# A decoder on one core: where the pieces of a norm and of an expert choice stand in a written order of matmuls

## The chip, the cores and the metric

The kernel is one launch on one core of a Trainium2 chip. The core has five engines that run side by side: TensorE (PE, matmuls and transposes; its weight loads are shown apart as PEld), VectorE (DVE), ScalarE (ACT), GpSimd (POOL) and SyncE (SP, which issues transfers). Each runs its own instructions in order, and they wait for each other through semaphores. Matmul results land in PSUM[...]; DVE and ACT copy them out[...]. The metric is the device time of the launch in microseconds (us), the median of a few runs.

## What is computed

Eight sequences of 512 tokens of width 256, with a context of 64 tokens each, go through two decoder layers. The change lies in the second one (Layer 1), in its attention over tokens and context, and in the choice of experts that follows:

```python
# Layer 1, second attention: 8 heads of 64, keys and values of the tokens and of the context together
q1, k1, v1 = x1 @ Wq1, x1 @ Wk1, x1 @ Wv1
k2, v2 = x2 @ Wk2, x2 @ Wv2
k, v = concat([k1, k2]), concat([v1, v2])            # 512 + 64 rows
attn = softmax(q1 @ k.T * 64 ** -0.5)
x = layernorm(x + (attn @ v) @ Wo + bo)

# Layer 1, experts: 8 of them, the best two per token
xn = layernorm(x) * gamma + beta
probs = softmax(xn @ router_w.T / 1.5)
w, idx = top_k(probs, 2)
y = silu(xn @ W1[e]) @ W2[e]                          # per expert e
out = sum over the two of w * y, + x                  # then once more: x = layernorm(x + out)
```

All data is float32.

## The kernel before

**Stages.** Layer 0's attentions and its feed-forward come first (0 to about 1500 us), then Layer 1's self-attention (to about 2109 us), the attention with the context (2109 to about 2885 us), the experts (to about 3410 us) and the final norms of the eight sequences (to the end).

**Who sets the order.** A planner orders each engine's instructions: it goes by readiness in its own estimate of the times, and among those that are ready by the order in which the program was written. It also hands out the buffers of a pool when the first writer of a tile is planned, and puts in the waits. Where the program says `tc.manual_schedule(engines={PE})`, PE keeps the written order; in the stage with the context this holds for PE alone. `keep_in_program_order` puts one instruction behind all that is written before it on its engine.

**The stage with the context** (L1531 on) goes over 128 units: sequence b, head pair c (0 to 3), query tile i (0 to 3, 128 rows each). `_pipeline` (L32) walks steps; at step s it calls, in this order, `l1x_scores` for unit s, `l1x_transposes` for unit s - 2, `l1x_values` for unit s - 6 and `l1x_ahead` for unit s. Then it takes one piece of work off the list `put_off`.

- `l1x_scores` (L1124): four products of q and k, one PSUM tile of two banks per head (`s_sc`, two buffers); then for each head DVE's negated row maximum (`nm`, L1138) and ACT's exponential with its row sum (`p`, L1139); then `scaled` (L915): DVE's reciprocal and two multiplications of p by it.
- `l1x_transposes` (L1145): nine transposes of p into three PSUM tiles of one bank (`tP2`, then `tP` twice), and their copies to SBUF with `evac` (L104), which takes DVE and ACT by turns.
- `l1x_values` (L1159): products of values and transposed p into one PSUM tile (`o_pv`), closed at the fourth query tile. After the fourth head pair `out_done` puts two pieces of the output projection (`o_out`) on the list, the second of which ends with `normed` (L206), the layer norm of the sequence. Then it calls `routed` (L1518).
- `l1x_ahead` (L1112): the next head pair's projections: q at i = 0 (`t_qk`, copied by ACT), k at i = 2 (copied by DVE), v at i = 3 (`t_v`, copied by ACT). At i = 1 there is none; there `x_transposed` makes the next sequence's transposed `xT` (c = 2, eight transposes `tT`, two PSUM tiles), or the context's values for two sequences (c = 1).

**PSUM** in this stage: two buffers `s` of two banks, three `t` of one bank, one `o`. All of `tP2`, `tP`, `t_qk`, `t_v`, `tT`, `tZ`, `o_out`, `o_r` and `o_rank` take a `t`.

**The route of a sequence** is what `routed` puts on the list, a piece per step: with the second projection piece `route_norm` (a second layer norm, into `z`, doubling of `xs[b]` and its transfer to `total`), a step with nothing, `route_transposes` (eight transposes `tZ` of z, ACT makes `xnT` of them), `route_odds` (16 small matmuls `o_r`, softmax), `route_picks` (the best two, `greatest` called twice), `route_places` (ranks `o_rank`, and eight indirect transfers of rows to `rows_in` by POOL). `xT` and `xnT` have the same tag, `xT`, in a pool with two buffers. For the last sequence the pieces go on `last_route`, which the pipeline of the experts takes up. After the last but one come `early_blocks` (DVE, tables for the experts) and the first expert's loads.

**A layer norm** (`normed`): per row tile DVE takes statistics (`st`, L213) and aggregates them (`mv`, L214), adds epsilon (`ve`, L215), POOL takes the power (`rs`, L216), and the scaling follows: DVE (L227), or with `on_act` one DVE instruction (L220, into `ve` again) and four of ACT (L224). With `then` given, the scaling is not written at once but put on that list.

Of the kernel before, what the change touches and what calls it, by code (L numbers as in the profile page):

```python
# [11 lines left out]
F32 = mybir.dt.float32  # L12
I32 = mybir.dt.int32
AF = mybir.ActivationFunctionType
ALU = mybir.AluOpType
# [9 lines left out]
NEG = -1.0e30  # L25
LN_EPS = 1e-5
PE = mybir.EngineType.PE
SLOT = 2048
TILES = 2

# [19 lines left out]
def decoder_kernel(ctx: ExitStack, tc: tile.TileContext, a: dict, out: bass.AP):  # L50
# [155 lines left out]
    def normed(dst, r, on_act=False, then=None):  # L206

        st = work.tile([P, NT, 6], F32, tag="st", name="st")
        mv = work.tile([P, NT, 2], F32, tag="mv", name="mv")
        ve = work.tile([P, NT], F32, tag="ve", name="ve")  # L210
        rs = work.tile([P, NT], F32, tag="rs", name="rs")
        for i in range(NT):
            dve.bn_stats(st[:, i, :], r[:, i, :])  # L213
            dve.bn_aggr(mv[:, i, :], st[:, i, :])  # L214
        dve.tensor_scalar(ve, mv[:, :, 1], LN_EPS, None, ALU.add)  # L215
        pool.tensor_tensor(rs, ve, mhalf, ALU.pow)  # L216

        def scaling(held=lambda instruction: instruction):
            if on_act:
                dve.scalar_tensor_tensor(ve, mv[:, :, 0], -1.0, rs, ALU.mult, ALU.mult)  # L220
            for i in range(NT):
                if on_act:
                    held(
                        act.activation(dst[:, i, :], r[:, i, :], AF.Identity, bias=ve[:, i : i + 1], scale=rs[:, i : i + 1])  # L224
                    )
                    continue
                dve.tensor_scalar(  # L227
                    dst[:, i, :], r[:, i, :], mv[:, i, 0:1], rs[:, i : i + 1], ALU.subtract, ALU.mult
                )

        if then is None:
            scaling()
        else:
            then.append(scaling)
# [1 line left out]
    def r_tile():  # L236
        return work.tile([P, NT, D], F32, tag="r", name="r", bufs=1)

    def project_and_norm(b, lhs, w, n, plus, later=None):

        r = r_tile()

        def piece(i2):
            o = u_tile("o_out").rearrange("p (i n) -> p i n", i=2)
            for j in range(2):
                i = 2 * i2 + j
                for c in range(n):
                    pe.matmul(  # L248
                        o[:, j, :],
                        lhsT=lhs[:, c, i * P : (i + 1) * P],  # L250
                        rhs=w[:, c, :],
                        start=(c == 0),
                        stop=(c == n - 1),
                    )
            dve.tensor_tensor(r[:, 2 * i2 : 2 * i2 + 2, :], o, plus[:, 2 * i2 : 2 * i2 + 2, :], ALU.add)
            if i2 == NT // 2 - 1:
                normed(xs[b], r)

        for i2 in range(NT // 2):
            if later is None:  # L260
                piece(i2)
            else:
                later.append(partial(piece, i2))
# [657 lines left out]

    put_off = []

    def l1_scores(b, c, m):
        q, k, _ = live["qkv", b, c]
        s = s_tile("s_sc")
        width = sum(i + 1 for i in GROUPS[m]) * P
        p = ph.tile([P, 2, width], F32, tag=f"p{m}", name="p")
        sums = col("sums", 4)
        at = 0  # L930
        for i in GROUPS[m]:
            n = (i + 1) * P
            for j in range(2):
                h = 64 * j
                pe.matmul(  # L935
                    s[:, j, at : at + n],
                    lhsT=q[h : h + 64, i * P : (i + 1) * P],
                    rhs=k[h : h + 64, 0:n],
                    start=True,
                    stop=True,  # L940
                )
            at += n
        at = 0
        for g, i in enumerate(GROUPS[m]):
            n = (i + 1) * P
            masked_softmax(
                s[:, :, at : at + n], p[:, :, at : at + n], causal[:, S - n : S], n, 1.0 / 8.0, sums, 2 * g
            )
            scaled(p[:, :, at : at + n], sums[:, 2 * g : 2 * g + 2], n)
            at += n  # L950
        live["p", b, c, m] = p
# [19 lines left out]
    def out_done(b, c, o, w, n, plus, then=None):  # L971
        if c == 0:
            live["aT", b] = big_tile("aT")
        aT = live["aT", b]
        evac(aT[:, c, :], o)
        if c == n - 1:
            project_and_norm(b, aT, w, n, plus(), put_off)
            if then:
                then(b)

# [143 lines left out]
    def l1x_scores(b, c, i):  # L1124
        q, k, _ = live["qkv", b, c]
        p = p_tile(S + S2, bufs=4)
        sums = col("sums", 4)
        nm = col("nm", 2)
        ss = [s_tile("s_sc")[:, :, 0:HALF] for _ in range(2)]
        for t in range(2):  # L1130
            for j, s in enumerate(ss):
                h = 64 * j
                at = S2 * (1 - j) + HALF * t
                pe.matmul(  # L1134
                    s[:, t, :], lhsT=q[h : h + 64, i * P : (i + 1) * P], rhs=k[h : h + 64, at : at + HALF], start=True, stop=True
                )
        for j, s in enumerate(ss):
            dve.tensor_reduce(nm[:, j : j + 1], s, AX.XY, ALU.max, negate=True)  # L1138
            act.activation(  # L1139
                p[:, j, :].rearrange("p (t n) -> p t n", t=2), s, AF.Exp, bias=nm[:, j : j + 1], accum_out=sums[:, j : j + 1]  # L1140
            )
        scaled(p, sums, S + S2)
        live["p", b, c, i] = p

    def l1x_transposes(b, c, i):  # L1145
        p = live.pop(("p", b, c, i)).rearrange("p j n -> p (j n)")
        if i == 0:
            live["pt", b, c] = pts[c % 2], ph.tile([P, S], F32, tag="pt2", name="pt2")
        pt, pt2 = live["pt", b, c]
        t = t_tile("tP2")[:, 0, :]  # L1150
        pe.transpose(t, p[:, S : S + P], ident)  # L1151
        evac(pt2[:, i * P : (i + 1) * P], t)
        for j in range(2):
            t = t_tile("tP")
            for k in range(NT):
                pe.transpose(t[:, k, :], p[:, (S + P) * j + k * P : (S + P) * j + (k + 1) * P], ident)  # L1156
            evac(pt[j][:, :, i * P : (i + 1) * P], t)

    def l1x_values(b, c, k):  # L1159

# [56 lines left out]
    def over_i(c):  # L1217
        return c.unsqueeze(1).to_broadcast([P, NT, NE])

    def route_norm(b):  # L1220
        z = keep.tile([P, NT, ROW], F32, tag="zr", name="z")
        normed(z[:, :, 0:D], xs[b])

        dve.tensor_scalar(xs[b], xs[b], 2.0, None, ALU.mult)
        sp.dma_start(out=total[b * S : (b + 1) * S, :].rearrange("(i p) d -> p i d", p=P), in_=xs[b])
        live["z", b] = z

    def route_transposes(b):
        z = live["z", b]
# [35 lines left out]
    def greatest(pick, left):  # L1265
# [6 lines left out]
        dve.tensor_tensor(pick, over_i(rev), over_e(top), ALU.is_equal)  # L1272
        return pick

    def route_picks(b):
        pr = live.pop(("pr", b))
        rest = e_tile("rest")
        picks = [greatest(e_tile("pick0"), pr)]
        dve.scalar_tensor_tensor(rest, picks[0], -2.0, pr, ALU.mult, ALU.add)
        picks.append(greatest(e_tile("pick1"), rest))  # L1280

        picked = work.tile([P, NT + 1, NE], F32, tag="both", name="both", bufs=1)
        pool.memset(picked[:, NT, :], 0.0)
        both, z = picked[:, 0:NT, :], live["z", b]
        dve.tensor_tensor(both, picks[0], picks[1], ALU.add)
        dve.tensor_tensor(z[:, :, D : D + NE], both, pr, ALU.mult)

        tc.keep_in_program_order(dve.tensor_copy(z[:, :, D + NE], tokens_at[:, b * NT : (b + 1) * NT]))
        live["picks", b] = picks, picked
# [226 lines left out]
    AHEAD = 1  # L1516

    def routed(b):  # L1518
        pieces = [partial(f, b) for f in (route_norm, route_transposes, route_odds, route_picks, route_places)]
        if b == NB - 1:  # L1520

            last_route.extend(pieces[:1] + 2 * [nothing] + pieces[1:])
            return

        product = put_off.pop()
        put_off.extend([lambda: (product(), pieces[0]()), nothing] + pieces[1:])
        if b == NB - 2:
            put_off.append(early_blocks)
            put_off.extend(partial(moe_load, n, tables_rows) for n in range(AHEAD))
# [1 line left out]
    with phase("l1_context") as ph, tc.manual_schedule(engines={PE}):  # L1531
        l1x_share(0)
        l1x_context_values(0)
        for what in range(3):
            l1x_project(0, 0, what)
        _pipeline(
            [(b, c, i) for b in range(NB) for c in range(4) for i in range(NT)],
            [(0, l1x_scores), (2, l1x_transposes), (6, l1x_values), (0, l1x_ahead)],
            put_off,
        )  # L1540

# [10 lines left out]
    halves = [h for _ in range(NB // 2) for h in slot("last").rearrange("p (b i d) -> b p i d", b=2, i=NT)]  # L1552
    for b in range(NB):
        sp.dma_start(out=halves[b], in_=total[b * S : (b + 1) * S, :].rearrange("(p i) d -> p i d", p=P))
    for b in range(NB):
        y = ph.tile([P, NT, D], F32, tag="y_out", name="y_out", bufs=4)
        normed(y, halves[b], on_act=True)
        act.dma_start(out=out[b].rearrange("(p i) d -> p i d", p=P), in_=y)


# [89 lines left out]
```

## Time and profile before

| | us |
|---|---|
| median of three runs | 3441.79 (3436.52 to 3451.23) |
| the profiled execution | 3444.91 |
| its span, first to last instruction | 3443.2 |
| busy: PE, DVE, ACT, POOL | 3283.1, 2064.1, 1514.2, 1068.8 |
| stage with the context (2109 to 2885): PE, DVE, ACT busy | 748.2, 536.8, 342.4 |
| of it: maxima (L1138), exponentials (L1139), scaling of p (L920) | 183.3, 189.7, 122.3 |
| of it: copies of 128x512 from `tP`, DVE (L108) and ACT (L110), 128 each | 87.1, 74.2 |
| of it: copies of 128x128 from `tP2`, DVE and ACT, 64 each | 18.0, 17.0 |

A line of the profile's timeline gives start, duration, engine, line, operation, what is written and read, shapes and count; in brackets how long the engine sat idle before it, and who ended that. In the table of windows a line has the stretch and its length, then busy time and count of PE, PEld, DVE, ACT and POOL, then the clock granted to TensorE as a share of full speed, the share of the DMA engines and GB/s.

### The profile page before, as it was taken

How to read it: one execution, taken by the hardware profiler on the slowest of the kernel's cores; microseconds unless marked ns; L12 is line 12 of the kernel's file. 1: busy time of each engine (PE TensorE's matmuls, PEld its weight loads, DVE VectorE, ACT ScalarE, POOL GpSimd, SP SyncE). 2: the span in 40 equal slices, each digit the busy share in tenths (PEclk: the TensorE clock that was granted, in tenths of full speed). 3: DMA queues.
4: the chain of work that ended last, by engine and by line, in shares of the span. 5: the costliest groups of instructions: out<-in, count | busy, mean ns of one | idle time of the engine just before them, and what ended most of it. 6: DMA issues, size and time to landing. Idle time of an engine off the chain costs nothing. (4 is left out here: it accounts for less than half of the span.)

```text
span 3443.2 us, 53163 instructions
## 1 busy us (share of the span) xinstructions
PE 3283.1 (95%) x19574; PEld 2083.5 (61%) x19574; DVE 2064.1 (60%) x6605; ACT 1514.2 (44%) x3140; POOL 1068.8 (31%) x1032
## 2 busy tenths in 40 slices
PE   8999999998999989999999999999999999999995
PEld 3444444446666656666676666555555556888884
DVE  5777777766666467777777775667776764111102
ACT  2444444453343245655556654444444443222222
POOL 3777777762111122222222220011111111222222
PEclk8999999998999999999999999999999999999998
DMA  4011011120000099323233230000000005666674
GB/s 136 27 25 34 24 38 38 41 63 13 2 2 1 1 241 255 57 35 40 38 44 44 38 50 4 4 20 19 23 20 15 15 19 191 188 187 185 187 232 136
DMA packets 166006, 235.00 MB, mean 68 GB/s; under 512 B 26569, under 2 KB 128649, under 8 KB 165746
## 3 DMA queue, kind: packets, MB, share of 16 engines
q1 hardware_dynamic: 139010, 175.83, 16.3%
q0 software_dynamic: 25584, 51.57, 10.5%
q10 hardware_dynamic: 1152, 4.19, 0.3%
q8 instruction: 155, 2.54, 0.3%
q14 instruction: 105, 0.86, 0.1%
HBM read 135.83 MB, written 61.11 MB: 57 GB/s over the span
## 5 line engine op out<-in xcount | busy, mean ns | idle before, releaser
L438 DVE CUSTOM_DVE_ANT_0 scored<-s_sc,decay 128x512 f32<-128x512 f32 x512 | 332.6, 687 | 192.2 <-PE s_sc L433 192.2
L290 ACT ACTIVATE p<-p,nm 128x384 f32<-128x384 f32 (+3 forms) x512 | 282.5, 553 | 259.0 <-DVE nm L279 259.0
L895 POOL DMA_DIRECT2D qk<-turned x256 | 204.1, 1223 | 583.4 <-PE s_sc L935 293.6
L496 ACT ACTIVATE pt<-s_st 128x1024 f32<-128x1024 f32 x256 | 262.0, 1024 | 269.3 <-PE s_st L492 242.8
L920 DVE TENSOR_SCALAR p<-p,rsum 128x576 f32<-128x576 f32 (+4 forms) x768 | 300.4, 434 | 10.2
L1506 DVE TENSOR_SCALAR y<-o_y,share 128x256 f32<-128x256 f32 x71 | 34.2, 484 | 403.1 <-PE o_y L1486 403.1
L1139 ACT ACTIVATE p<-s_sc,nm 128x576 f32<-128x576 f32 x256 | 189.7, 743 | 195.2 <-DVE nm L1138 173.5
L1469 PE MATMUL s_h<-xnT,we 128*128 128x256 f32 (+1 forms) x1248 | 258.8, 361 | 0.0
L279 DVE CUSTOM_DVE_ANT_0 p<-s_sc,tabs 128x384 f32<-128x384 f32 (+3 forms) x512 | 225.1, 484 | 46.4 <-PE s_sc L935 44.3
L1486 PE MATMUL o_y<-we,h 128*128 128x256 f32 x1136 | 251.4, 379 | 0.0
L1486 PEld LDWEIGHTS o_y<-we,h 128*128 128x128 f32 x1136 | 215.3, 190 | 29.0
L1507 POOL DMA_INDIRECT total<-y,to x71 | 110.3, 1553 | 385.7 <-DVE y L1506 172.2
L1469 PEld LDWEIGHTS s_h<-xnT,we 128*128 128x128 f32 x1248 | 215.4, 190 | 23.9 <-ACT xnT L1448 0.2
L1138 DVE TENSOR_REDUCE nm<-s_sc 128x1 f32<-128x576 f32 x256 | 183.3, 749 | 77.7 <-PE s_sc L1134 76.6
L110 ACT COPY pt<-tP 128x512 f32<-128x512 f32 (+1 forms) x224 | 110.0, 491 | 216.7 <-PE tP L1151 119.3
L935 PE MATMUL s_sc<-qk 64*128 64x384 f32 (+3 forms) x1024 | 179.4, 462 | 15.5 <-DMA qk<-turned 10.3
L968 ACT COPY pt<-tP 128x384 f32<-128x384 f32 (+1 forms) x384 | 167.0, 527 | 56.1 <-PE tP L967 55.9
L967 PEld LDWEIGHTS tP<-ident,p 128*128 128x128 f32 x1280 | 141.3, 141 | 52.3 <-issue 30.8
L1134 PE MATMUL s_sc<-k,q 64*128 64x288 f32 x1024 | 166.3, 437 | 3.3 <-ACT p L1139 3.1
L967 PE MATMUL tP<-ident,p 128*128 128x128 f32 x1280 | 163.2, 278 | 3.4 <-ACT pt L968 2.4
L433 PE MATMUL s_sc<-k,q 32*128 32x512 f32 x1024 | 156.7, 654 | 3.0 <-ACT k L418 1.5
L450 DVE TENSOR_SCALAR_CACHE_REDUCE diag<-scored,mx 128x128 f32<-128x128 f32 x512 | 155.8, 342 | 0.0
(281 smaller groups left out, 6444.9 us busy)
## 6 DMA issues: line engine op xcount, KB each, us to landing
we<-in_mo_w SPq DMA_DIRECT2D x78, 1024.0 KB
rows_in<-zero SPq DMA_DIRECT2D x64, 530.0 KB
qk<-turned POOLq DMA_DIRECT2D x256, 128.0 KB, 4.6
coef<-in_ff_upw SPq DMA_DIRECT2D x40, 256.0 KB
coef<-in_ff_dnw SPq DMA_DIRECT2D x40, 256.0 KB
xr<-rows_in SPq DMA_DIRECT2D x32, 265.0 KB
x<-in_x SPq DMA_DIRECT2D x8, 512.0 KB
total<-x SPq DMA_DIRECT2D x8, 512.0 KB
```

What stands on the lines that cost most here:

```text
L279: dve.tensor_tensor_reduce(out=p[:, j, 0:n], in0=s[:, j, 0:n], in1=m, scale=-scale, scalar=3.0e38, op0=ALU.add, op1=ALU.min, accum_out=nm[ ...
L290: act.activation(p[:, j, 0:n], p[:, j, 0:n], AF.Exp, bias=nm[:, j : j + 1], scale=-1.0, accum_out=sums[:, at + j : at + j + 1],)
L438: dve.tensor_tensor_reduce(out=scored[:, h, :], in0=s[:, j, :], in1=decay[:, i, :], scale=1.0, scalar=-3.0e38, op0=ALU.mult, op1=ALU.max, ...
L496: tc.keep_in_program_order(act.activation(pt, s, AF.Exp, scale=1.0 / 16.0))
L895: pool.dma_start(out=qk[h : h + 32], in_=other[g : g + 32], accum_op=ALU.add)
L920: dve.tensor_scalar(p[:, j, 0:n], p[:, j, 0:n], rsum[:, j : j + 1], None, ALU.mult)
L935: pe.matmul(s[:, j, at : at + n], lhsT=q[h : h + 64, i * P : (i + 1) * P], rhs=k[h : h + 64, 0:n], start=True, stop=True,)
L967: pe.transpose(t[:, n, :], p[:, j, at * P : (at + 1) * P], ident)
L1138: dve.tensor_reduce(nm[:, j : j + 1], s, AX.XY, ALU.max, negate=True)
L1139: act.activation(p[:, j, :].rearrange("p (t n) -> p t n", t=2), s, AF.Exp, bias=nm[:, j : j + 1], accum_out=sums[:, j : j + 1])
L1469: pe.matmul(s[:, j, :], lhsT=w1[:, c, f * P : (f + 1) * P], rhs=xnT[:, c, :], start=(c == 0), stop=(c == KC - 1),)
L1486: pe.matmul(o, lhsT=h[:, f, i * P : (i + 1) * P], rhs=w2[:, f, :], start=(f == 0), stop=(f == 7),)
```

## The change

Nothing is computed otherwise, and the number of matmuls, copies and transfers stays. What moves:

- `project_and_norm` and `route_norm` hand `normed` a list, so that the scalings are pieces of their own. `routed` puts more pieces on the list: scaling of `xs[b]`, `route_norm` (statistics of z alone), scaling of z, transposes together with the doubling of `xs[b]` (`route_twice`), odds, the first choice (`route_pick`), the second, places. For the last sequences some are joined again.
- `scaled` is a stage of its own, `l1x_scaled`, for unit s - 1.
- ACT copies `tP2` and the first `tP`, DVE the second, in each step.
- In a step `l1x_ahead` comes before `l1x_values`.
- In the final norms DVE keeps the written order, and the scaling of a sequence is written after the statistics of the next.
- `scaling` passes its DVE multiplications through `held`, as it did ACT's; `route_scale` gives `keep_in_program_order` for it, so these multiplications stand behind all DVE work that is written before them.

```diff
                     continue
-                dve.tensor_scalar(
-                    dst[:, i, :], r[:, i, :], mv[:, i, 0:1], rs[:, i : i + 1], ALU.subtract, ALU.mult
+                held(
+                    dve.tensor_scalar(
+                        dst[:, i, :], r[:, i, :], mv[:, i, 0:1], rs[:, i : i + 1], ALU.subtract, ALU.mult
+                    )
                 )
...
-    def project_and_norm(b, lhs, w, n, plus, later=None):
+    def project_and_norm(b, lhs, w, n, plus, later=None, then=None):
...
-                normed(xs[b], r)
+                normed(xs[b], r, then=then)
...
+    then_scaled = None
...
-            project_and_norm(b, aT, w, n, plus(), put_off)
+            project_and_norm(b, aT, w, n, plus(), put_off, then_scaled)
...
+        live["p", b, c, i] = p, sums
+
+    def l1x_scaled(b, c, i):
+        p, sums = live["p", b, c, i]
         scaled(p, sums, S + S2)
-        live["p", b, c, i] = p
...
-        evac(pt2[:, i * P : (i + 1) * P], t)
+        act.copy(pt2[:, i * P : (i + 1) * P], t)
...
-            evac(pt[j][:, :, i * P : (i + 1) * P], t)
+            (act.copy, dve.tensor_copy)[j](pt[j][:, :, i * P : (i + 1) * P], t)
...
+    then_scaled = []
+
+    def route_scale(b):
+        then_scaled.pop(0)(tc.keep_in_program_order)
+
     def route_norm(b):
         z = keep.tile([P, NT, ROW], F32, tag="zr", name="z")
-        normed(z[:, :, 0:D], xs[b])
+        normed(z[:, :, 0:D], xs[b], then=then_scaled)
+        live["z", b] = z
+
+    def route_twice(b):
 
         dve.tensor_scalar(xs[b], xs[b], 2.0, None, ALU.mult)
         sp.dma_start(out=total[b * S : (b + 1) * S, :].rearrange("(i p) d -> p i d", p=P), in_=xs[b])
-        live["z", b] = z
...
+    def route_pick(b):
+        live["pick", b] = [greatest(e_tile("pick0"), live["pr", b])]
+
     def route_picks(b):
-        pr = live.pop(("pr", b))
+        pr, picks = live.pop(("pr", b)), live.pop(("pick", b))
         rest = e_tile("rest")
-        picks = [greatest(e_tile("pick0"), pr)]
...
     def routed(b):
-        pieces = [partial(f, b) for f in (route_norm, route_transposes, route_odds, route_picks, route_places)]
+        def both(f, g):
+            return lambda b: (f(b), g(b))
+
+        pieces = [
+            route_scale,
+            route_norm,
+            route_scale,
+            both(route_transposes, route_twice),
+            route_odds,
+            route_pick,
+            route_picks,
+            route_places,
+        ]
+        if b >= NB - 2:
+
+            pieces[5:7] = [both(*pieces[5:7])]
+            pieces[0:2] = [both(*pieces[0:2])]
         if b == NB - 1:
-
-            last_route.extend(pieces[:1] + 2 * [nothing] + pieces[1:])
+            pieces[0:2] = [both(*pieces[0:2])]
+        pieces = [partial(f, b) for f in pieces]
+        if b == NB - 1:
+
+            last_route.extend(pieces)
             return
-
-        product = put_off.pop()
-        put_off.extend([lambda: (product(), pieces[0]()), nothing] + pieces[1:])
+        put_off.extend(pieces)
...
-            [(0, l1x_scores), (2, l1x_transposes), (6, l1x_values), (0, l1x_ahead)],
+            [(0, l1x_scores), (2, l1x_transposes), (1, l1x_scaled), (0, l1x_ahead), (6, l1x_values)],
...
-    for b in range(NB):
-        y = ph.tile([P, NT, D], F32, tag="y_out", name="y_out", bufs=4)
-        normed(y, halves[b], on_act=True)
-        act.dma_start(out=out[b].rearrange("(p i) d -> p i d", p=P), in_=y)
+    then = []
+    with tc.manual_schedule(engines={DVE}):
+        for b in range(NB + 1):
+            if b < NB:
+                live["y", b] = ph.tile([P, NT, D], F32, tag="y_out", name="y_out", bufs=4)
+                normed(live["y", b], halves[b], on_act=True, then=then)
+            if b:
+
+                then.pop(0)()
+                act.dma_start(out=out[b - 1].rearrange("(p i) d -> p i d", p=P), in_=live["y", b - 1])
```

More of the change, by code (lines that the diff above doesn't have):

```diff
@@ L27 @@
 PE = mybir.EngineType.PE
+DVE = mybir.EngineType.DVE
 SLOT = 2048
@@ L1141, in l1x_scores @@
             )
+        live["p", b, c, i] = p, sums
+    def l1x_scaled(b, c, i):
+        p, sums = live["p", b, c, i]
         scaled(p, sums, S + S2)
-        live["p", b, c, i] = p
     def l1x_transposes(b, c, i):
-        p = live.pop(("p", b, c, i)).rearrange("p j n -> p (j n)")
+        p = live.pop(("p", b, c, i))[0].rearrange("p j n -> p (j n)")
         if i == 0:
```

## The prediction, written before the changed kernel ran

> **What bounds the kernel now.** I read the page first (span, busy shares, the chain), then the windows of the stage that the diff touches, then its timeline and waits.
>
> ```profile
> span 3443.2 us, 53163 instructions
> PE 34%; DVE 4%; DMA 1%; POOL 1%; ACT 1%; issue 1%; SPq 0%; DVEq 0%; POOLq 0%; ACTq 0%
> ...
> 2109.00:2885.00 776.00, 748.21 (x4123) 435.47 (x4122) 536.79 (x1321) 342.35 (x813) 101.86 (x143) 0.98 0.06 19
> ```
>
> The last line is the context stage, 2109 to 2885 us: PE busy 748 of 776 us, DVE 537, ACT 342. PE sets the pace, so an edit there is worth only what it does to PE's gaps. Its steps are seen by the starts of `s_sc` in the timeline. Undisturbed ones last 5.23 us (i = 0, 2), 4.32 (i = 1, no projection) and 5.29 (i = 3), the same to 0.01 us wherever nothing is put off into them. The route of batch b falls into the steps of batch b+1; +n is the step for unit n of that batch.
>
> ```profile
> 2229.02 1.24 PE L1134 MATMUL s_sc<-k,q 64*128 64x288 f32 x8
> 2230.55 0.27 ACT L110 COPY pt<-tP 128x128 f32<-128x128 f32 x1 [5.77 <-PE tP L1151]
> 2234.31 1.24 PE L1134 MATMUL s_sc<-k,q 64*128 64x288 f32 x8
> 2238.86 1.38 DVE L227 TENSOR_SCALAR z<-x,mv,rs 128x256 f32<-128x256 f32 x4 [0.90 <-POOL rs L216]
> 2242.09 0.88 DVE L108 COPY pt<-tP 128x128 f32<-128x128 f32 x2
> 2242.43 1.97 PE L1234 MATMUL tZ<-ident,z 128*128 128x128 f32 x8 [2.82 <-DVE pt L108]
> 2244.33 2.29 PE L1134 MATMUL s_sc<-k,q 64*128 64x288 f32 x8
> 2251.59 1.85 PE L1249 MATMUL o_r<-rw,xnT 128*128 128x8 f32 x16
> 2253.37 1.24 PE L1134 MATMUL s_sc<-k,q 64*128 64x288 f32 x8
> 2253.53 0.59 ACT L110 COPY xT<-tT 128x512 f32<-128x512 f32 x1 [4.00 <-PE o_r L1249]
> 2262.82 2.05 PE L1101 MATMUL t_v<-v_k,xT 128*128 128x128 f32 x16 [0.84 <-DVE pt L108]
> ```
>
> For b = 0: +7 starts at 2229.02 and lasts 5.29, +8 10.02, +9 9.04. What PE needs in +8 is 5.23 + 0.96 for eight tZ transposes (0.11 apart) = 6.19, so 3.83 is lost: both norms' stats and scalings run on DVE there, the copies that free transposing buffers come late, and tZ waits. In +9 PE needs 4.32 + 0.96 (tT) + 1.75 (o_r) = 7.03; the other 2.0 are the clock:
>
> ```profile
> 2238.30:2241.70 3.40, 1.31 (x4) 0.24 (x2) 2.84 (x7) 0.70 (x2) 0.53 (x1) 1.00 0.00 0
> 2241.70:2245.10 3.40, 2.67 (x12) 2.21 (x14) 2.39 (x6) 2.90 (x7) 0.00 (x0) 0.50 0.44 154
> ...
> 2828.80:2832.20 3.40, 1.82 (x14) 1.38 (x16) 3.23 (x8) 2.87 (x7) 0.00 (x0) 1.00 0.43 154
> ```
>
> (PE busy is the second number, granted clock the third from the end.) After 1.31 busy of 3.40 us the clock is halved; 1.82 busy kept it. In +11, t_v waits 0.92 for a DVE copy. The same sums for the seven routed batches, from their own step starts: 6.8, 6.8, 3.2, 3.2, 6.9, 5.3, 4.4 = **36.5 us**. That, and some 5 us where the stage fills and drains, is all PE time to be had: the ceiling is about 1.1% of the span.
>
> **The change, part by part.** It adds and removes no matmul, copy or transfer; it moves them.
>
> *Norms and choice in more pieces.* xs is scaled at +7 (4 x 0.35 = 1.39), stats of z at +8 (about 1.8), z scaled at +9 (1.38), doubled at +10 (0.69). A step's own DVE work is about 3.4 (nm 1.42, copies 0.8, reciprocal and scaling 1.15), so each fits its 5.2-us step. The scalings are held behind the step's own DVE work and may wait there for POOL's rs (0.9 in the row of 2238.86); behind them in DVE's queue is the next step's nm, not due before 1.27 of that step, so this is covered; uncovered it would be 0.9 a scaling, 13 in all. tZ, now at the end of +10, finds z done and buffers free: the 36.5 go, in the first place.
>
> *What is late next.* `xT` and `xnT` share a tag with two slots. In before, xnT(b) was made at +8 and read by o_r at +9; xT(b+2), also due at +9, had to wait for it: that is the wait of 4.00 us of the xT copy for o_r above. It did not take xT(b+1)'s slot, which t_v still read at 2262.82 (+11). Now xT(b+2) is made at +9 and takes the free slot; xnT(b) at +10 finds the other held by xT(b+1) until the t_v of +11. So two tZ tiles stand in two of the three `t` buffers through step +11, and its transposes go through one. Times from the start of the step: tP2 1.17; its ACT copy ends 1.80 (the row of 2230.55: 1.53 + 0.27); first tP 1.88 to 2.5; its copy comes behind the first exponential:
>
> ```profile
> 2399.51 1.24 PE L1134 MATMUL s_sc<-k,q 64*128 64x288 f32 x8
> ...
> 2401.64 0.74 ACT L1139 ACTIVATE p<-s_sc,nm 128x576 f32<-128x576 f32 x1 [3.19 <-DVE nm L1138]
> 2402.37 0.58 ACT L110 COPY pt<-tP 128x512 f32<-128x512 f32 x1
> ```
>
> that is, 2.86 to 3.44; second tP 3.5 to 4.1; DVE copy 0.68 to 4.82; t_v 4.88 in place of 2.25: 2.63 late. Then ACT makes xnT (2 x 0.78) while PE has 1.0 us of values: o_r, now at the end of +11, is 0.75 late. Together 3.4, six times (b = 0 to 5; there is no xT(8)): **20.3**. From below: 0, if the slots are given otherwise than I read; from above 4.1 each (24.6), if the second exponential goes before the copy.
>
> *Its clock.* From 1.28 to 4.88 PE runs 0.9 of transposes, and later 0.75 idle beside o_r, whose 8-column matmuls fill little. The Trainium skill (TensorE: Matmul & The Clock Gate, Why this matters for your kernels) says that the clock falls with idle gaps of over some 3 us between bursts; no single gap here is over 1.2, so by the rule this costs 0. By the row above 2.1 us missing from one window is enough, and about half of the possible alignments have that. I take the row: one halved window of 3.4 us a conflict, costing PE 1.2 of its busy time, 7; none to 19 (two windows each, as after 2242). For b = 6 0.8: a sparse o_r has the clock fall by itself half the time.
>
> *Projections ahead of values.* A projection now comes at 2.25 and needs tP2's buffer, free at 1.80: nothing, 0.45 in hand. At +9 the two tT come at 2.25 and 2.69; the second needs a buffer free at 3.44 (ACT) or 3.4 (DVE). Before, 1.0 us of values covered that. 0.75 x 7 = **5.3**, 0 if ACT takes the copy ahead of the exponential.
>
> *Copies by place.* ACT gets 64 small copies more (0.27 each, 17 us of its 430 idle), DVE 64 fewer. Nothing, as long as they stay ahead of the exponentials in ACT's queue. *Later scaling*: it only gives the DVE scaling of a step the lower rank; p is read a step later still. 0; the planner may leave it where it is.
>
> *Queues.* The last transfer of `total` moves two steps on SP, with nothing behind it. The eight indirect stores of a batch hold POOL 23.6 us (2852.59 to 2876.18 for b = 6); POOL's copies into k behind them have over a step in hand, and the next xb and rs come at +21. For b = 6 the places come one step (3.5 us) later, and xr and the first weights follow on SP: xr was ready some 6 us before PE wanted it, the first weights 4. +0.5, from 0 to 4.
>
> *Final norms.*
>
> ```profile
> 3417.74 2.07 ACT L224 ACTIVATE y_out<-last,ve,rs 128x256 f32<-128x256 f32 x4 [23.26 <-DVE ve L220]
> ...
> 3435.41 0.17 DVE L215 TENSOR_SCALAR ve<-mv 128x4 f32<-128x4 f32 x1 [0.32 <-ACT y_out L224]
> ```
>
> DVE now runs in written order. A norm's stats take 4 x 0.52 (0.43 from stats to their own aggregate, 0.10 on) + 0.2; two come before the first output, which starts near 3418.9. `ve` has two buffers, so that L215 of b+2 waits for ACT's outputs of b, with L220 of b+1 behind it: a round is about 2.46 us, where ACT alone needs 2.0. The last output starts near 3436.0, before at 3437.4: **-1.3** (-4 to +1).
>
> The sum: -36.5 + 20.3 + 7 + 0.8 + 5.3 + 0.5 - 1.3 = **-3.9**. The profiled execution took 3444.9 (span 3443.2, 1.7 around it): 3441.0. The median of the runs shown is 3441.8: **3438**.
>
> **The rivals.** *No conflict of slots*: -36.5 + 0.8 + 5.3 + 0.5 - 1.3 = -31, 3411. For it: I infer slots from one pair of waits, addresses are not in the trace. Against: two readers held the two slots at once in before, and the third waited for just one of them. *Half of it* (conflict short, clock kept): about -20, 3422.
>
> *ACT's order, the slower side.* All small copies now sit in ACT's queue, whose order is the planner's. If tP2's copy is planned behind the first exponential it ends at 2.86 + 0.27 = 3.13 and each of 94 projections starts 0.9 late: +85, 3523. It decides from 0.18 each, a copy that ends at 2.43. Against: in all but a few of the 64 steps that had it on ACT it started at 1.53. *The conflict at its dearest*: 24.6 with 19 of clock: +12, and with 4 at the hand-over +16 to +20, 3460.
>
> *Nothing gained because DVE's backlog only moves*: the stalls return at +8 with stats of z before nm. 3442, same side as the forecast.
>
> **How the numbers follow.** Forecast 0.45 (its own range 3425 to 3452), backlog only moved 0.05, no conflict 0.18, half of it 0.10, dearest conflict 0.12 and ACT's order 0.10. 0.5% (17 us) is about what a measurement can tell from no change. Faster: 0.28. Same: 0.50. Slower: 0.22. The range, 3406 to 3466, takes in the no-conflict case and the dearest conflict and leaves out ACT's order and what lies beyond.
>
> **What would show it.** Right: +8 at 5.23; tZ without a wait; at +11 ACT's xnT waiting for t_v, PE's tP and t_v waiting for pt copies, the step over 10 us; seven steps +9 near 6.0. Wrong: xnT made within +10, so that only the gain is left; or PE waits for ACT's pt in every step.

## The result, and the profile after

The changed kernel took **3450.85 us** (median of 12 runs, 3442.62 to 3459.90), the kernel before 3443.18 (12 runs beside it): ratio 1.0022, 95% interval 1.0014 to 1.0031. That is some 8 us (5 to 11) longer; the forecast was 3438, 4 us shorter. The difference is within the half per cent that the prediction calls no change, and the time within its range, but the change lies on the other side of zero. The profiled execution of after (span 3458.2, whole time 3459.9) is the longest of its runs, and 3 us of that were lost before the context stage began. So stages are compared below, not spans.

The head of the page of after, as shown of before:

```profile
span 3458.2 us, 53253 instructions
PE 3291.4 (95%) x19574; PEld 2095.2 (61%) x19574; DVE 2052.5 (59%) x6541; ACT 1524.3 (44%) x3202; POOL 1067.2 (31%) x1032
PE 35%; DVE 3%; ACT 2%; POOL 1%; DMA 1%; issue 0%; ACTq 0%; POOLq 0%; DVEq 0%; SPq 0%
...
2112.40:2887.20 774.80, 749.34 (x4123) 440.89 (x4122) 522.36 (x1257) 355.17 (x877) 100.77 (x143) 0.98 0.05 17
```

PE still bounds. The last line is the window of the context stage: 774.8 us where before had 776.0. By the counts 64 operations went from DVE to ACT, the small copies: DVE is busy 14 us less, ACT 13 more. A stage that was to lose 36.5 us of stalls and gain some 33 looks as if nothing had happened. Yet its steps changed much, and so did the hand-over behind it, from the last projection to the experts' first `o_y`.

By the starts of `s_sc`, the last `o_out`, and the first and the last `o_y` in the profiled executions (us; for the three steps of a route the last column has the forecast length, else the forecast difference):

| | before | after | forecast |
|---|---|---|---|
| first `s_sc` to last `o_out` (stage) | 776.15 | 774.80 | -3.1 |
| last `o_out` to first `o_y` (hand-over) | 18.06 | 32.12 | +0.5 |
| first to last `o_y` (experts) | 499.81 | 500.11 | 0 |
| last `o_y` to the end | 39.87 | 38.80 | -1.3 |
| an undisturbed step, i = 0 / 1 / 2 / 3 | 5.23 / 4.32 / 5.23 / 5.29 | 5.03 / 4.32 / 5.03 / 5.10 | 0 |
| step +8, batches 0 to 6 | 8.72 to 10.05 | 5.03 to 5.24 | length 5.23 |
| step +9, batches 0 to 5 | 7.03 to 9.11 | 7.06 | length 6.03 |
| step +11, batches 0 to 5 | 6.31 to 7.22 | 10.17 to 12.69 | length over 10 |

The timeline of after around the route of batch 0:

```profile
2237.63 1.24 PE L1139 MATMUL s_sc<-k,q 64*128 64x288 f32 x8
...
2241.11 1.41 DVE L1143 TENSOR_REDUCE nm<-s_sc 128x1 f32<-128x576 f32 x2
...
2244.04 1.23 PE L1139 MATMUL s_sc<-k,q 64*128 64x288 f32 x6 [0.46 <-ACT p L1144]
...
2247.29 0.66 PE L199 MATMUL tT<-ident,x 128*128 128x128 f32 x4 [0.45 <-ACT pt L1165]
...
2254.93 1.09 PE L1249 MATMUL tZ<-ident,z 128*128 128x128 f32 x8
...
2255.95 1.24 PE L1139 MATMUL s_sc<-k,q 64*128 64x288 f32 x8
...
2257.81 0.66 PE L1164 MATMUL tP<-ident,p 128*128 128x128 f32 x4 [0.36 <-ACT pt L1160]
...
2259.71 0.66 PE L1164 MATMUL tP<-ident,p 128*128 128x128 f32 x4 [1.25 <-ACT pt L1165]
...
2261.16 3.10 PE L1106 MATMUL t_v<-v_k,xT 128*128 128x128 f32 x16 [0.78 <-DVE pt L1165]
...
2264.29 1.45 ACT L1250 ACTIVATE xnT<-tZ,gb 128x512 f32<-128x512 f32 x2 [3.90 <-PE t_v L1106]
```

`tZ` no longer waits (2254.93): the stall of +8 is gone. The step from 2255.95 is +11. Its transposes go through one buffer, each `tP` waits for the copy of the one ahead, `t_v` comes 5.21 after the step's start (forecast 4.88), and only when `t_v` has read xT does ACT make `xnT`: the conflict of slots, place for place as forecast. Not in the forecast is the row of 2241.11: in +8 nm starts 3.48 after its `s_sc`, where 1.27 is usual, and the scores of +9 wait for the exponential behind it (2244.04).

The clock by windows in the same step +11:

```profile
2258.53:2261.93 3.40, 1.43 (x11) 1.20 (x12) 1.60 (x5) 1.87 (x5) 0.00 (x0) 1.00 0.01 2
2261.93:2265.33 3.40, 3.40 (x16) 2.32 (x14) 0.23 (x1) 1.04 (x2) 0.00 (x0) 0.50 0.00 0
```

No gap in the first is over 1.25 us, and still the next runs at half clock. The rule that the prediction weighed (the Trainium skill, TensorE: Matmul & The Clock Gate, Why this matters for your kernels: gaps of over some 3 us) would have had no such window; the row of before was the better guide. Busy time is not the whole of it either. In before a window in which PE is busy all the time, with 16 `o_r` (8 columns each) in it, is followed by half clock too:

```profile
2835.65:2839.06 3.41, 3.41 (x27) 2.68 (x26) 2.15 (x8) 0.30 (x2) 0.00 (x0) 1.00 0.00 0
2839.06:2842.47 3.41, 3.41 (x13) 1.86 (x13) 2.81 (x9) 2.42 (x6) 0.00 (x0) 0.50 0.02 5
```

Behind the stage, the PE timelines of before and then of after, from the last `o_out`:

```profile
2885.69 0.38 PE L1447 MATMUL tZ<-ident,xr 128*128 128x128 f32 x2
2887.00 1.95 PE L1469 MATMUL s_h<-xnT,we 128*128 128x256 f32 x8
...
2894.51 1.18 PE L1234 MATMUL tZ<-ident,z 128*128 128x128 f32 x8
...
2903.53 7.07 PE L1486 MATMUL o_y<-we,h 128*128 128x256 f32 x32
```

```profile
2895.62 2.19 PE L1249 MATMUL tZ<-ident,z 128*128 128x128 f32 x8 [8.09 <-DVE z L229]
...
2898.04 3.83 PE L1264 MATMUL o_r<-rw,xnT 128*128 128x8 f32 x16
...
2902.61 1.06 PE L1486 MATMUL s_h<-xnT,we 128*128 128x256 f32 x2
```

The scaling that completes z of the last sequence starts 8.0 us after the last `o_out` in both (DVE timeline of before, then of after):

```profile
2893.48 1.38 DVE L227 TENSOR_SCALAR z<-x,mv,rs 128x256 f32<-128x256 f32 x4 [1.06 <-POOL rs L216]
```

```profile
2895.16 1.38 DVE L229 TENSOR_SCALAR z<-x,mv,rs 128x256 f32<-128x256 f32 x4 [1.06 <-POOL rs L217]
```

Before, PE filled this time with `s_h` of the first expert. After, the transposes of z stand first in PE's queue, PE waits 8.09 us, and then runs at half clock (the 16 `o_r` take 3.83 us, 1.95 in the stage). The first `s_h` comes 15.4 us after the last `o_out`, before 1.5.

### The profile page after: what moved, and what is told of

Same layout as the page of the kernel before. It is cut to its first block, busy times and chain, and to the rows that moved or that the text cites. A ratio compares the mean times of both kernels' runs of the same rounds, so it can differ in the third digit from the quotient of the medians.

```text
span 3458.2 us, 53253 instructions
## 1 busy us (share of the span) xinstructions
PE 3291.4 (95%) x19574; PEld 2095.2 (61%) x19574; DVE 2052.5 (59%) x6541; ACT 1524.3 (44%) x3202; POOL 1067.2 (31%) x1032
## 5 line engine op out<-in xcount | busy, mean ns | idle before, releaser
L940 PE MATMUL s_sc<-qk 64*128 64x512 f32 (+3 forms) x1024 | 179.1, 460 | 15.8 <-DMA qk<-turned 10.6
L1160 ACT COPY pt<-tP 128x128 f32<-128x128 f32 x128 | 34.1, 266 | 283.8 <-PE tP L1159 283.8
L1139 PEld LDWEIGHTS s_sc<-k,q 64*128 64x128 f32 x1024 | 94.5, 189 | 104.3 <-ACT p L1144 37.5
```

Source lines behind the costliest of these rows:

```text
L1139: pe.matmul(s[:, t, :], lhsT=q[h : h + 64, i * P : (i + 1) * P], rhs=k[h : h + 64, at : at + HALF], start=True, stop=True)
```

## The experiments

The theory from this profile: two losses, the slots (+27 to 33) and the hand-over (+14), eat up what the stalls gave back, and with it a gain of 0.2 us in each plain step that was not forecast. Rivals: the step +11 is slow from the order of PE's work; the hand-over is late because batch 6's places, and behind them tokens and weights of the first expert, come late.

**Own slots for xnT.** The tile goes where a weight lay whose use is over by then (the trace calls it v_k):

```diff
-        xnT = work.tile([P, KC, S], F32, tag="xT", name="xnT")
+        xnT = wk2 if b < NB - 1 else work.tile([P, KC, S], F32, tag="xT", name="xnT")
```

> The changed kernel, but xnT of the first seven sequences is written over wk2, whose last reader is done before the stage's first step, so it needs no slot of the tag xT. Slots theory: steps +11 fall from 10.2 to 12.7 us to 6.9 (5.10 + 1.78 of o_r), the four steps +12 of 6.6 to 5.03, about 33 us in all; the hand-over to the experts stays as it is, so the time is the changed kernel's less 33: 3418. Rival, the stall at +11 comes from the planner's order on ACT and DVE and not from the slots: steps +11 stay over 10 us, 3450.

3421.29 us, ratio to before 0.9944 (0.9923 to 0.9964): 29.6 below after. The six steps +11 that were long last 6.98, the stage 745.34. Rows of its timeline at the same place:

```profile
2247.36 1.44 ACT L1250 ACTIVATE v_k<-tZ,gb 128x512 f32<-128x512 f32 x2 [1.31 <-PE tZ L1249]
...
2247.69 1.24 PE L1139 MATMUL s_sc<-k,q 64*128 64x288 f32 x8
...
2249.03 1.04 PE L1164 MATMUL tP<-ident,p 128*128 128x128 f32 x8
...
2249.90 1.95 PE L1106 MATMUL t_v<-v_k,xT 128*128 128x128 f32 x16
```

ACT starts on the transposing buffers 0.3 before the step begins and is done 1.1 into it, ahead of the step's own large transposes, and `t_v` comes at 2.21. The slots cost **29.5 us** of stage with their share of the clock (forecast 27.3). The hand-over stays at 31.6.

**Places of batch 6 a step earlier.**

```diff
+        if b == NB - 2:
+            product, first = put_off.pop(), pieces.pop(0)
+            put_off.append(lambda: (product(), first()))
```

> The changed kernel, but for the last sequence that is routed in this stage the first scaling and the statistics of z go with the second projection piece again, so that its transposes, odds, picks and places come one step earlier (places at +11, as before the change). Hand-over theory: the first expert's rows and weights are read some 4 us earlier, land before the second expert's loads are issued, and PE's wait of some 14 us between the last projection and the first expert's product shrinks to a few: 3438 to 3443. Rival, the wait is not set by when the places come (a slower indirect transfer, SP's order): no change, 3450.

3452.07 (1.0024; 1.0014 to 1.0034). The hand-over is 31.46, the wait for z 8.09 as in after: late places do not cause it. And batch 6, packed again as before, stalls again (8.11 and 7.83 at +8 and +9).

**Values first again, in the kernel after.**

```diff
-            [(0, l1x_scores), (2, l1x_transposes), (1, l1x_scaled), (0, l1x_ahead), (6, l1x_values)],
+            [(0, l1x_scores), (2, l1x_transposes), (1, l1x_scaled), (6, l1x_values), (0, l1x_ahead)],
```

> The changed kernel with values ahead of the next projections again, nothing else undone. If the 0.20 us by which plain steps became shorter (5.23 to 5.03, 5.29 to 5.10) come from the order of matmul shapes on PE, they are lost again: about 93 steps by 0.2 = 19 us, less seven tT waits of 0.8: 3464. Rival, the shorter steps come from the copies by place or the later scaling: plain steps stay at 5.03, 3445.

3454.88 (1.0036; 1.0021 to 1.0050). Plain steps are back at 5.23 and 5.29, so the 0.2 us is the order of the products; +9 falls from 7.06 to 6.35, which is the wait of the second `tT` (forecast 0.75); +11 falls to 10.33 in five of six batches; the stage stays at 774.95. Inside after, the order saves some 10 us in plain steps and gives as much back: 5 where the second `tT` waits and 4 in the steps +11.

**Projections ahead of values alone, in the kernel before.**

```diff
-            [(0, l1x_scores), (2, l1x_transposes), (6, l1x_values), (0, l1x_ahead)],
+            [(0, l1x_scores), (2, l1x_transposes), (0, l1x_ahead), (6, l1x_values)],
```

> The kernel before with the projections ahead of the values, nothing else. By the order of shapes: plain steps 5.03 and 5.10, -19, tT waits +5, the stalls of the routed steps as before: 3429. Rival, the buffers: with copies by turns tP2's copy is in DVE's queue in half the steps and ends at 2.9, so that half the projections wait 0.6 for their buffer: +28, 3455 or more.

3470.55 (1.0080; 1.0056 to 1.0104): 27 longer, the rival's number. Half of the plain steps with a projection last 5.87 or 5.94; rows of its timeline in one of them:

```profile
2170.86 0.74 ACT L1139 ACTIVATE p<-s_sc,nm 128x576 f32<-128x576 f32 x1 [2.44 <-DVE nm L1138]
...
2171.35 0.88 DVE L108 COPY pt<-tP 128x128 f32<-128x128 f32 x2
...
2171.68 1.98 PE L1088 MATMUL t_qk<-xT,q_k 128*128 128x512 f32 x4 [0.57 <-DVE pt L108]
```

The small copy stands behind nm in DVE's queue there, and the projection, now early, waits for that copy's buffer.

**Copies by place alone, in the kernel before.**

```diff
-        evac(pt2[:, i * P : (i + 1) * P], t)
+        act.copy(pt2[:, i * P : (i + 1) * P], t)
...
-            evac(pt[j][:, :, i * P : (i + 1) * P], t)
+            (act.copy, dve.tensor_copy)[j](pt[j][:, :, i * P : (i + 1) * P], t)
```

> The kernel before with the copies by place alone (pt2 always by ACT, the first large copy by ACT, the second by DVE). Theory that this part is worth nothing by itself: plain steps stay at 5.23, 4.32, 5.23 and 5.29 us, the stage at 776, the time at 3443 (-3 to +3). Rival, DVE relieved of 64 small copies scales z sooner at +8: stalls of +8 and +9 shrink by up to 1.5 us a batch, -10, 3433. Other rival, the small copy behind the first exponential in ACT's queue: tP starts late in every step, over 3460.

3438.97 (0.9990; 0.9977 to 1.0002): not told from no change; stage 772.87, plain steps as before.

**Projections ahead of values and copies by place, in the kernel before.**

> The kernel before with the copies by place and the projections ahead of the values, nothing else. Theory (with the small copy always done early by ACT, the projection's buffer is free when it comes): every plain step 5.03 (4.32 for i = 1), about 93 x 0.20 = 19 us saved, less up to 5 for the two tT of seven steps +9: 3424 to 3432. Rival, the steps of 5.87 seen with the order alone have another cause than the small copies on DVE: they remain, time near 3465. Second rival, the order's gain is eaten by the stalls at +8 and +9 that stay in: 3443.

3424.28 (0.9957; 0.9944 to 0.9970). Every plain step with a projection is 5.03 or 5.10, none 5.87; the stage is 755.97, **16.9 below** the copies alone, 13.3 of it in plain steps, although +8 and +9 still stall (8.3 to 9.3 and 8.0 to 9.0). PE's rows of a plain step of before, and then of one of this run, in the timeline:

```profile
2166.62 1.04 PE L1156 MATMUL tP<-ident,p 128*128 128x128 f32 x8
2167.59 1.08 PE L1168 MATMUL o_pv<-pt,vc 128*64 128x512 f32 x4
2168.60 1.98 PE L1088 MATMUL t_qk<-xT,q_k 128*128 128x512 f32 x4
2170.51 1.24 PE L1134 MATMUL s_sc<-k,q 64*128 64x288 f32 x8
```

```profile
2161.28 1.04 PE L1156 MATMUL tP<-ident,p 128*128 128x128 f32 x8
2162.15 1.88 PE L1088 MATMUL t_qk<-xT,q_k 128*128 128x512 f32 x4
2163.97 1.08 PE L1168 MATMUL o_pv<-pt,vc 128*64 128x512 f32 x4
2164.97 1.24 PE L1134 MATMUL s_sc<-k,q 64*128 64x288 f32 x8
```

From start to start, `tP` takes 0.97 before and 0.87 here, `t_qk` 1.91 and 1.82, `o_pv` 1.01 and 1.00. With the projection next to the transposes, of the same 128*128 shape, PE changes to the 64-wide shape once less between full-width products. That this change costs the 0.1 at either end is read from the rows and was not measured by itself; that the order gives the 0.2 is shown by this run and by values first.

**Two empty steps back in the last sequence's route, in the kernel after.** Before had them between its norm and its transposes; after had dropped them.

```diff
-            last_route.extend(pieces)
+            last_route.extend(pieces[:1] + 2 * [nothing] + pieces[1:])
```

> The kernel after with two empty steps put back between the first and the second piece of the last sequence's route, as before had them. Theory (the last route's transposes are put ahead of the first expert's products in PE's order and wait there for z on DVE): PE's wait of 8.09 us for z and the half clock after it go, from the last projection to the first o_y 18 us in place of 32, time 3451 - 13 = 3437. Rival, the hand-over is late because tokens and weights of the first expert come late: no change, 3451. In between, 3444, if the wait goes but the clock still falls.

3444.38 (1.0016; 1.0007 to 1.0025). The hand-over is 17.90, the wait for z and the half clock are gone. By the medians 6.5 came back, not 13, and the interval of the ratio overlaps that of after. The experts last 505.0 in place of 500.1; the first row shows the transposes of z without a wait, the second has most of that loss (PE timeline):

```profile
2888.89 1.11 PE L1249 MATMUL tZ<-ident,z 128*128 128x128 f32 x8
...
2970.68 0.66 PE L1464 MATMUL tZ<-ident,xr 128*128 128x128 f32 x2 [5.81 <-DMA xr<-rows_in]
```

The first expert that takes tokens of the last sequence waits for them. In after that wait is 2.85, in before 1.79. The stores of these tokens begin 61.9 us after the last `o_out` here, 43.3 in after and 59.2 in before; why 2.7 later than in before, with the same empty steps, stays open. From the last `o_out` to the last `o_y` it is 517.9 in before, 532.2 in after, 522.9 here.

**Own slots and the two empty steps.**

> The kernel after with both amendments: own slots for the normed rows of the route (the first run of the last set) and the two empty steps of the last route. Theory that the two losses are independent: 3421 - 13 = 3408, stage 745, last projection to first o_y 18. Rival, with the stage shorter the last route's z is late for another reason and the hand-over stays at 32: 3421.

3414.86 (0.9931; 0.9909 to 0.9953); stage 745.55, hand-over 18.93, last `o_out` to last `o_y` 521.0. The stage keeps the first gain and the hand-over the second. In the time the second is some 6, half of the forecast here too, and the interval overlaps that of own slots alone.

**Own slots and one empty step.**

> The kernel after with own slots for the normed rows of the route and one empty step (not two) between the first and the second piece of the last sequence's route. Two empty steps leave PE a wait of 2.6 to 5.8 us for the tokens of a later expert, because the last route's stores come late. Theory that this wait is the other side of the same delay: with one empty step it goes to 0, the transposes still stand behind products of the first expert, from the last projection to the first o_y some 18 to 21 us; time 3415 - 3 = 3412 (3408 to 3415). Rival, the wait for the tokens is a matter of transfers and stays: 3415 to 3418, and PE waits for z again.

3409.14 (0.9900; 0.9883 to 0.9916); last `o_out` to last `o_y` 519.4. The time came in as expected (3408 to 3415), the reason only in part: PE waits 2.06 for z and 1.89 for the tokens, not 0 for both (PE timeline):

```profile
2857.85 0.67 PE L1249 MATMUL tZ<-ident,z 128*128 128x128 f32 x4 [2.06 <-DVE z L229]
...
2923.53 0.41 PE L1464 MATMUL tZ<-ident,xr 128*128 128x128 f32 x2 [1.89 <-DMA xr<-rows_in]
```

**The empty steps taken out of the kernel before, nothing else.**

```diff
-            last_route.extend(pieces[:1] + 2 * [nothing] + pieces[1:])
+            last_route.extend(pieces)
```

> The kernel before with the two empty steps of the last sequence's route taken out, nothing else. Theory that the loss at the hand-over is this edit alone: a wait of PE of about 8 us for z, half clock after it, from the last projection to the first o_y 31 to 32 us in place of 18; in the profile +14 there and -2 at the wait for a later expert's tokens; time 3443 + 4 to 12. Rival, the loss needs the rest of the change (the split pieces, the held scalings): 18 stays, 3443.

3457.14 (1.0036; 1.0019 to 1.0053), 12 above the before beside it (3445.04). Hand-over 31.38, and the rows of after are there, in the PE timeline of a kernel that has nothing else of the change:

```profile
2888.86 2.19 PE L1234 MATMUL tZ<-ident,z 128*128 128x128 f32 x8 [8.08 <-DVE z L227]
...
2891.28 3.83 PE L1249 MATMUL o_r<-rw,xnT 128*128 128x8 f32 x16
```

**Fewer stats of z** (own slots, two empty steps; the normed rows' mean and variance are taken from one row tile of four, the others get copies of it, so the work left out is 1.4 us of DVE a batch). The rest of step +9 was open: 7.06 against 6.03 forecast.

```diff
-    def normed(dst, r, on_act=False, then=None):
+    def normed(dst, r, on_act=False, then=None, tiles=NT):
...
-            dve.bn_stats(st[:, i, :], r[:, i, :])
-            dve.bn_aggr(mv[:, i, :], st[:, i, :])
+            if i < tiles:
+                dve.bn_stats(st[:, i, :], r[:, i, :])
+                dve.bn_aggr(mv[:, i, :], st[:, i, :])
+            else:
+                pool.tensor_copy(mv[:, i, :], mv[:, 0, :])
...
-        normed(z[:, :, 0:D], xs[b], then=then_scaled)
+        normed(z[:, :, 0:D], xs[b], then=then_scaled, tiles=1)
```

> The kernel after with own slots for the normed rows and two empty steps, and the stats of z in the context stage taken on one of the four row tiles only (three stats and three aggregates, some 1.4 us of DVE, left out; the others get a copy of the first by POOL). Theory that the 1.0 us a batch which +9 lasts over the forecast comes from these stats standing ahead of nm in DVE's queue: +9 of seven batches 7.06 -> 6.03 (the wait of two tT of 0.75 left in), stage 745.5 - 8 = 738. Rival, it is the exponential's place in ACT's queue: 7.06 stays, 745.

A miss: +9 is 6.90 to 6.93, stage 742.58 (738 expected), time 3416.07 in one run. nm of +8 still starts 3.14 after its `s_sc`. But 0.5 of this the edit brought in itself: ahead of nm DVE now waits for POOL's copies.

```profile
2236.59 0.17 DVE L219 TENSOR_SCALAR ve<-mv 128x4 f32<-128x4 f32 x1 [0.52 <-POOL mv L218]
2236.67 1.41 DVE L1146 TENSOR_REDUCE nm<-s_sc 128x1 f32<-128x576 f32 x2
```

So this run does not say what the stats are worth. It leaves the scaling of xs ahead of them, with the scaling of p behind it, which keeps DVE busy into +8.

**xs scaled one step later** (own slots, one empty step):

```diff
         pieces = [
+            nothing,
             route_scale,
             route_norm,
             route_scale,
             both(route_transposes, route_twice),
             route_odds,
-            route_pick,
-            route_picks,
+            both(route_pick, route_picks),
             route_places,
         ]
...
```

> The kernel after with own slots for the normed rows, one empty step in the last sequence's route, and xs scaled in step +8 instead of +7 with all that follows one step later (choice of both experts in one step again, so that the places stay at +14). Theory that the surplus of +8 (0.2) and +9 (1.0) comes from the scaling of xs, held until POOL's rs and 1.4 us long, with the scaling of p and the stats of z behind it, all ahead of the next nm: +8 5.03, +9 6.03 in six batches (the two-tT wait of 0.75 left in), stage 745.5 - 7 = 738, time 3409 - 8 = 3401. Rival, the backlog only moves to +10: the same sum, 3409.

DVE's and PE's rows around the start of +8, batch 0, in its timeline:

```profile
2232.59 0.95 DVE L923 TENSOR_SCALAR p<-p,rsum 128x576 f32<-128x576 f32 x2
2233.02 1.24 PE L1139 MATMUL s_sc<-k,q 64*128 64x288 f32 x8
2233.46 1.38 DVE L229 TENSOR_SCALAR x<-r,mv,rs 128x256 f32<-128x256 f32 x4
...
2235.41 1.41 DVE L1143 TENSOR_REDUCE nm<-s_sc 128x1 f32<-128x576 f32 x2
```

3405.40 (0.9899; 0.9873 to 0.9924). The scaling of p now comes ahead of that of xs and is done 0.5 into the step, nm starts 2.39 after its `s_sc` in place of 3.48; +8 is 5.03, +9 6.22 to 6.25, the stage **737.93** (738 expected, 745.51 in the run with one empty step). The DVE backlog is the cause, and it did not move on to +10 (5.03); which of its parts weighs most is not separated, as all that follows in the route moved with the scaling. That the stage met the number is in part chance: +8 and +9 of the six batches give 6.1 of the 7.6, the steps behind them 3.9 more, and the steps ahead of and behind the six routes take 2.4 back (2.9 of it lies in the third step of the stage, which varies between executions). In the time, 3405.4 against 3409.1, it can't be told apart from the run with one empty step (ratios 0.9899 and 0.9900, on two chips). It is the lowest time here, 1.0% below before; from the last `o_out` to the last `o_y` it took 522.9 in its profile, 3.5 more than the run with 3409, and why stays open.

## Why the prediction was wrong, step by step

| step of the sum | forecast, us | what the runs show | from |
|---|---|---|---|
| stalls of +8 and +9 | -36.5 | gone; +8 never over 5.24 | after |
| conflict of slots and its clock | +27.3 | +29.5 | own slots against after, stage |
| projections ahead of values, plain steps | 0 | -13.3 (the whole stage -16.9) | order with copies, against copies alone |
| second `tT` at +9 | +5.3 | 0.71 a batch, some 5 | after against values first |
| scalings held behind the step's DVE work | 0 | +6.1 | xs a step later, steps +8 and +9 |
| last sequence's route | inside +0.5 | +14.1 at the hand-over | hand-over of after; alone, +13.3 in before |
| final norms | -1.3 | -1.1 | last `o_y` to the end |

**The step that failed** is the hand-over, +0.5 under *Queues*; it measured +14.1. The sum priced only batch 6's places and the first expert's transfers there, and took no notice that the last sequence's pieces, put on a list of their own, lose the two empty steps that stood between its norm and its transposes. Those steps did no work, but they set the order on PE: without them the transposes of z stand ahead of the first expert's products, which had covered the 8 us in which DVE and POOL make z. With this step right the sum is some 10 above before, where the medians have 8. Taken out of before alone, the two empty steps cost 12 us (7 to 18).

**Right by luck, from errors that nearly cancel,** is the stage: -3.1 forecast, -1.35 measured. Missed was a gain (13.3, the plain steps), because the projection's move was priced by its waits only, with the products' own durations taken as fixed. Missed was a loss: the sum called the wait of the held scalings "covered" up to 1.27 of the next step, and put the cover's end at 0.9 a scaling, 13 in all. The row of before had the parts (POOL's rs late, 1.38 of scaling, then 1.1 for p, and the stats of z among them), and only in their sum does nm start 3.48 into the step. In six batches +8 loses 0.2 and +9 0.8 by it, 6.1 in all, half of the price named. So the rival "DVE's backlog only moves" (stats of z before nm, in +8) came true in small. With the table's terms the stage comes to some -9. Two more are seen: +2.8 in the third step of the stage (4.74 before, 7.56 after, and between 4.74 and 7.80 in the other executions, whatever the kernel) and some +2 at +14 (the places' steps last 6.24 to 6.69, where 5.03 and the 1.0 that the places cost in before's +11 make 6.0). Some 3 us of the stage are not assigned.

**Right**: the bound (PE, by waits that end at its queue), the slots that were inferred from one pair of waits, the place of every wait in +11, the size of the `tT` wait, the final norms, copies by place worth nothing alone. The six steps +11 average 11.34; the need of 6.85 (5.10 and 1.75 of `o_r`) and the forecast loss of 4.55 make 11.40. A little short was the clock: one halved window of 1.2 us of PE a conflict was forecast, the window shown cost 1.7 (all of 3.40 busy at half clock). In four batches +12 is long too (6.60 to 6.66 in place of 5.03), but not for the slots alone: with own slots it is 6.66 to 6.71 in 5 of the 24 such steps of four runs, each time right behind the `o_r` of +11. The rival "no conflict" would have been 3411; with the slots mended the kernel still took 3421, with the loss at the hand-over in it. The rival "ACT's order" did not come: the small copy stands ahead of the exponential in all plain steps.

## What to carry to other kernels

An empty step, or a piece's place on a list, is a statement about order: before it is dropped, look which engine's queue it sorts, and what had run in the time that the next piece must wait. A move that is priced by waits alone can miss that the products' own time changes with their neighbours, and a cost called "covered" has to be summed over all that the cover must take in one step, not piece by piece. When a change of several parts comes out near zero, take it apart: here the parts stood at -36, +29, -13, +6, +5 and +14, and with the two large losses mended the same change is 1.0% faster than before.

## What the runs showed of the hardware

The order of products changes PE's time with no wait in it: 5.23 to 5.03 us a step, with the 128*128 products together and the 64-wide ones behind them; which change of shape costs it was not measured. The clock fell to half after a window in which PE was busy 1.43 of 3.40 us though no gap exceeded 1.25 us, and also after one that was busy throughout, with 16 `o_r` of 8 columns in it. And the path through the last sequence's stores to the tokens of a later expert was closer to the end of its cover than the page of before told: PE's wait for them was 1.8 us in before, 2.8 in after, and 5.8 with the two empty steps back in.
